# A recurrent block (autocorrelation gather and LoRA feed-forward) on one core: earlier gather sums, searches ahead of outputs, LoRA's copies and w2's sums in other places

## The chip, the cores and the metric

The kernel runs on one NeuronCore of a Trainium2 chip. The metric is the device time in microseconds (us). Five engines work side by side, each through its own instructions in their written order: TensorE (PE, matrix products), VectorE (DVE), ScalarE (ACT), GpSimd (POOL, which also issues the indirect DMAs) and SyncE (SP, which issues the other DMAs). They wait for one another by semaphores.

## The reference

`x` is (2, 2048, 1024) in f32, that is 4096 rows of 1024.

```
xn = (x - mean) / sqrt(var + 1e-5)                    # per row
corr = irfft(|rfft(xn)|^2)                            # autocorrelation of each row
weights, delay = top_k(corr, 6)
s = sum_k softmax(weights)_k * roll(xn, -delay_k)     # "aggregate"
w(q) = tile(q, (1, 4));  lin(v) = v @ w.T + 0.5 * v @ A.T @ B.T   # rank 2
g = silu( lin2( silu(lin1(xn)) * lin3(xn) ) )         # hidden width 2752
out = x + s * g
```

The weights are tiled four times along their input, so the kernel folds the four parts of the input (or, for w2, of the output columns) before it multiplies.

## The kernel before

**Macros and steps.** The rows are taken in 8 macros of 512 rows (4 blocks r of 128). Each macro goes through 15 steps. Steps 0 to 9 (`up`) make the gated products of the hidden width: 5 chunks c in two pairs, with the matmuls of L556 into PSUM banks gu, a silu on ACT (L561), a product with the other half on DVE (z, L563) and sums over z on POOL (zf, L566 and L568). Step 10 (`up_rest`) makes the last, half-wide chunk: gu by L585 and L592, z by ACT (L602) and DVE (L603), sums on POOL (L607, L608) and DVE (L609). Steps 11 and 13 (`down_head`, q = 0 and 1: two row blocks each) and 12 and 14 (`down_tail`) make the down product y from seven sub-products p1 to p7 (L641) of sums of weights (B, and T1 to T4) and sums of zf (S1, S2, S4, made by `mix` on POOL, L633 to L636), then the `plain` products of the half-wide chunk (L651), silu (L722), the product with s (DVE, L723), the sum with x (POOL, L724) and the store (L725). Four y banks are used for each q; the fourth, y11, takes the bank that gu of the second unit of step 10 had, and p7 is the first product written to it.

**What runs beside.** While a macro's products run, the next macro is prepared: loads of x, statistics (L185 to L193), norm (L200 to L207, then yc and bcs, L145 and L134), a save of xn into a scratch in DRAM (twice in a row, so that a roll is one contiguous read), `turn` (transposes on PE, L230), at steps 9 and 10 `power` (the transform: waves fe and fo on PE, L384; ec, e2 and o2 on ACT; bT and its like on DVE, L394, and POOL, L395 and L398), and at steps 11 to 14 `lags` (corr by L426 to L443) and `search` (the six largest, their places and exponentials; L451, L453 on DVE, e by L462 on POOL). A search gives six gathers of `Gathers`: at most four rolls are in flight, by indirect DMA from POOL (L486), in five buffers. The first roll of a row block is scaled on ACT (L500), the other five are added on DVE (L503).

**What sets the order.** The program is written out by hand: program order is the order on each engine. `plan` gives each step lists of calls: `pre` ahead of its products, `mid` between them, `half` behind `mid`, and `end`; and `sums[p]`, how many gather sums are made at half and at the end of step p. `Gathers.begin` issues rolls ahead of each step and behind the sums at half. In `down_tail`, `between` stands between the outputs of the first and the second half of the columns. Two sums of each macro's r = 3 come behind its outputs, in step 1 of the next macro.

**Other names of the change.** `mix_weights`: four subtractions over w2 on POOL (L163 to L166), once, in macro 0. `lora_mid` (L611): four small sums into the half-wide chunk's zf and a copy on ACT (L619). `flush`: matmuls u of LoRA (L539) that were put off. `again` and `lora_spread`: one matmul u (L258), four copies on ACT and three DMAs on SP (rows, second) for the next macro. Buffer rings: tags "x" and "s" have three 128x1024 buffers each.

Sums at (half, end) before: steps 0 to 14 of the later macros (0,0) (1,1) (1,0) (1,0) (1,0) (1,0) (1,0) (2,1) (2,1) (2,1) (0,0) (1,0) (1,0) (2,1) (3,0).

Of the kernel before, what the change touches and what calls it, by code (L numbers as in the profile page):

```python
# [68 lines left out]
def block_kernel(ctx: ExitStack, tc: tile.TileContext, x, w13t, w0t, w5t, w2t, a13, b13, b5, a2t, tf, ti, pick, out):  # L69
# [78 lines left out]
    def fold_lora(nat):  # L148
# [11 lines left out]
    B = lambda k, n: w2_sb[:, :4, :].rearrange("p (a k) l -> p a k l", k=2)[:, :, k, n * 512 : (n + 1) * 512]  # L160
    T1, T2, T3, T4 = B(0, 1), t_sb[:, 0], t_sb[:, 1], t_sb[:, 2]
    mix_weights = [
        lambda: nc.gpsimd.tensor_tensor(T3, B(1, 1), B(0, 1), ALU.subtract),  # L163
        lambda: nc.gpsimd.tensor_tensor(T1, B(0, 1), B(0, 0), ALU.subtract),
        lambda: nc.gpsimd.tensor_tensor(T2, B(1, 1), T1, ALU.subtract),
        lambda: nc.gpsimd.tensor_tensor(T4, B(1, 0), T2, ALU.subtract),  # L166
    ]


# [305 lines left out]
    class Gathers:  # L475
# [16 lines left out]
        def sum(self, count):  # L492
            for _ in range(count):
                if not self.flying:
                    self.begin()
                st, r, k, g = self.flying.pop(0)
                w = st.w[:, r, k : k + 1]
                if k == 0:
                    s = self.s[st.m, r] = p3.tile([P, L], F32, tag="s", name=f"s_{st.m}_{r}")
                    nc.scalar.activation(s, g, AF.Copy, scale=w)  # L500
                else:
                    s = self.s[st.m, r]
                    nc.vector.scalar_tensor_tensor(s, g, w, s, ALU.mult, ALU.add)  # L503


    class Ffn:
# [69 lines left out]
        def up_rest(self, mid, half):  # L576

            st = self.st
            self.seed(4 * FULL + 2)
            self.seed(4 * FULL + 3)  # L580
            accs = [self.accs.pop(4 * FULL + j) for j in range(4)]
            for pair in range(2):
                js = (2 * pair, 2 * pair + 1)
                for j in js:
                    nc.tensor.matmul(  # L585
                        accs[j], lhsT=w5_sb[:, 1, j, :], rhs=st.yT[:, 1, :], start=False, stop=False, skip_group_check=True
                    )

                for j in js:
                    for wi, y in enumerate((st.yT[:, 0, :], st.yU)):  # L590
                        at = slice(64 * wi, 64 * wi + 64)
                        nc.tensor.matmul(  # L592
                            accs[j][at, :], lhsT=w5_sb[:, 0, j, at], rhs=y, start=False, stop=True, skip_group_check=True
                        )
                if pair == 0:
                    self.flush()
                    mid()
                    half()
            zs = self.zs[FULL] = []
            for j, acc in enumerate(accs):  # L600
                z = p5.tile([P, NR], F32, tag="z", name=f"z_{self.m}_{FULL}_{j}")
                nc.scalar.activation(z[:64, :], acc[:64, :], AF.Silu)  # L602
                nc.vector.tensor_tensor(z[:64, :], z[:64, :], acc[64:, :], ALU.mult)  # L603
                zs.append(z)
            self.late.append(lambda: self.a2(FULL, zs, 64))
            last = self.sum_of(FULL)
            nc.gpsimd.tensor_tensor(last[:64, :], zs[0][:64, :], zs[1][:64, :], ALU.add)  # L607
            nc.gpsimd.tensor_tensor(last[:64, :], last[:64, :], zs[2][:64, :], ALU.add)  # L608
            nc.vector.tensor_tensor(last[:64, :], last[:64, :], zs[3][:64, :], ALU.add)  # L609

        def lora_mid(self):  # L611

            self.flush()
            last = self.zf[FULL]
            for j in range(4):
                nc.vector.scalar_tensor_tensor(
                    last[0:2, :], self.u2[32 * j : 32 * j + 2, :], 0.5, last[0:2, :], ALU.mult, ALU.add
                )
            nc.scalar.copy(last[64:, :], last[:64, :])  # L619
# [41 lines left out]
        def down_head(self, q, mid, half):  # L661

            self.q, self.xs = q, {}
            for i, n in ((0, 0), (1, 0), (0, 1)):
                self.load_x(i, n)
            self.rc = [slice((2 * q + i) * P, (2 * q + i + 1) * P) for i in range(2)]
            A = lambda i, k: [self.zf[2 * a + k][:, self.rc[i]] for a in range(2)]
            S = [[t[:, 2 * a + q, :] for a in range(2)] for t in self.S]
            both = lambda t: [t[:, a, :] for a in range(2)]
            self.forms = [  # L670
                list(zip(lhs, both(rhs)))
                for lhs, rhs in (
                    (A(0, 0), B(0, 0)), (A(0, 1), B(1, 0)), (S[2], B(1, 1)), (A(1, 1), T4), (S[0], T1), (S[1], T2), (A(1, 0), T3),
                )
            ]
            p1_, p2_, p3_, p4_, p5_, p6_, p7_ = self.forms

            self.ys = [full(f"y_{self.m}_{2 * q + i}_{n}") for n in range(2) for i in range(2)]
            y00, y10, y01, y11 = self.ys
            self.add_to(y01, p1_, True)  # L680
            nc.scalar.copy(y00, y01)
            self.add_to(y11, p7_, True)
            self.p7 = p5.tile([P, NR], F32, tag="z", name=f"p7_{self.m}_{q}")
            nc.scalar.copy(self.p7, y11)
            self.add_to(y01, p6_)
            nc.vector.tensor_tensor(y10, y01, self.p7, ALU.add)
            if q == 0:
                self.lora_mid()
            mid()
            half()  # L690
            self.add_to(y00, p2_)
            self.add_to(y00, self.plain(0, 0))
# [35 lines left out]
    def plan(m, st, nxt, after, gathers, ffn_next):  # L728

        pre, mid, half, end = ([[] for _ in range(STEPS)] for _ in range(4))  # L730
        first = m == 0
        sums = [(1, 0)] * 7 + [(1, 2)] * 3 + [(1, 1), (0, 0), (2, 1), (2, 1), (0, 0)]
        sums[10] = (0, 0)
        sums[0], sums[1] = (0, 0), (1, 1)
        sums[7:10] = [(2, 1)] * 3
        sums[11:] = [(1, 0), (1, 0), (2, 1), (3, 0)]
        between = lambda: None
        if first:
            sums = [(0, 0)] * 7 + [(1, 1), (2, 1), (1, 2), (2, 2), (2, 1), (1, 0), (2, 1), (3, 0)]
            for p, f in enumerate(mix_weights):  # L740
                half[6 + p].append(f)
            mid[0].append(st.odd_first)
            pre[1].append(lambda: st.power(2))
            mid[1].append(lambda: st.power(3))
            for r in range(RT):
                look(st, r, mid[2 + r], end[2 + r], gathers)
            mid[2 + RT].append(st.weights)
            for c in range(2, FULL + 1):
                pre[(0, 0, 1, 3)[c - 2]].append(lambda c=c: load_first(c))
                end[2 * c - 3].append(lambda c=c: lessen_part(c))  # L750
        else:
            end[0].append(st.weights)
        if nxt is not None:
# [17 lines left out]
            mid[9].append(lambda: nxt.power(1))  # L771
            pre[10].append(lambda: nxt.power(2))
            mid[10].append(lambda: nxt.power(3))
            pre[11].extend([nxt.again, nxt.lora_spread])
            for r in range(RT):
                look(nxt, r, mid[MID + 1 + r], end[MID + 1 + r], gathers)
            mid[STEPS - 1].insert(0, lambda: ffn_next.seed(0, (0,)))
            between = lambda: (ffn_next.seed(0, (1,)), ffn_next.seed(1, (0,)))
            end[STEPS - 1].insert(0, lambda: ffn_next.seed(1, (1,)))
        for a in range(2):  # L780
            end[8 + a].append(lambda a=a: ffns[m].mix(a))
        if after is not None:
            pre[MID + 2].append(lambda: after.load(0))
            pre[MID + 4].append(lambda: after.load(1))
# [25 lines left out]
    with tc.manual_schedule():  # L810
# [73 lines left out]
        for m in range(macros):  # L884
# [3 lines left out]
            for p in range(STEPS):  # L888
                for f in pre[p]:
                    f()  # L890
                gathers.begin()
                middle = lambda p=p: [f() for f in mid[p]]

                def others(p=p):
                    gathers.sum(sums[p][0])
                    if sums[p][0]:
                        gathers.begin()
                    for f in half[p]:
                        f()

                if p < MID:
                    ffn.up(p // 2, p % 2, middle, others)
                elif p == MID:
                    ffn.up_rest(middle, others)
                else:
                    q, part = divmod(p - MID - 1, 2)
                    if part == 0:
                        ffn.down_head(q, middle, others)
                    else:
                        s = lambda i, q=q: gathers.s[m, 2 * q + i]  # L910
                        ffn.down_tail(middle, others, s, between if q else lambda: None)
                gathers.sum(sums[p][1])
                for f in end[p]:
                    f()
# [111 lines left out]
```

## Time and profile before

| | |
|---|---|
| runs | 1174.82, 1176.18, 1178.7 us (median 1176.18) |
| profiled execution | 1179.55 us, span of its instructions 1177.7 us |
| mean granted PE clock | 0.987 |
| VectorE L503 (gather sums) | 158, 237.1 us busy, 1.28 us median |
| POOL L486 (rolls) | 192, 240.1 us busy |
| PE L556 (up products) | 1280 matmuls, 626.7 us busy |
| macro 1, 216.9 to 358.5 us | 141.6 us, PE busy 138.72 |
| macro 7, 1046.0 to 1177.7 us | 131.7 us, PE busy 121.39 |

A row of a timeline has the start, the length (of a run of equal instructions), the engine, the line, the operation with the names of its output and inputs, shapes, and a count; in square brackets stands how long the engine sat idle before it and what ended that. A list of waits has, for an engine's line and the one that released it, the total, the number and the longest. A row of a window table has, behind its stretch in us, its length, then busy time and count of PE, weight loads, DVE, ACT and POOL, then the granted PE clock, the DMA share and GB/s. A matmul of 512 columns starts 0.429 us behind the last one in a dense stretch; its listed length overlaps the next.

### The profile page before, as it was taken

What the parts mean: (1) busy time and instruction counts of PE and PEld (TensorE: products, weight loads), DVE (VectorE), ACT (ScalarE), POOL (GpSimd) and SP (SyncE); (2) the same over time, 40 slices, a digit from 0 to 9 for tenths busy, and PEclk for the clock granted to TensorE, in tenths of its full rate; (3) what the DMA queues carried; (4) which work ended last, traced back from release to release, by engine and by line L of the source; (5) the groups of instructions that cost most, each with busy time, mean ns of one, the idle gap of its engine ahead of it and who ended that gap; (6) DMA issues with size and microseconds to landing.
All of it is one profiled execution on the core that took longest, in us unless ns stands there. A gap on an engine that the chain in (4) does not pass through costs nothing.

```text
span 1177.7 us, 11263 instructions
## 1 busy us (share of the span) xinstructions
PE 1120.5 (95%) x3476; PEld 472.5 (40%) x3476; DVE 758.2 (64%) x1122; ACT 619.5 (53%) x1077; POOL 779.3 (66%) x659
## 2 busy tenths in 40 slices
PE   5999879999999999899999999999999999999996
PEld 4344234443343434344343433434334443344432
DVE  5589467765586647766487655866557865574454
ACT  4656523666346663465635665355643666345531
POOL 4667967548666585666956568665767648665663
PEclk9999989999999999999999999999999999999998
DMA  9841357543475334654356544554446543363335
GB/s 364 372 163 54 92 203 239 198 143 111 156 225 203 130 124 160 230 187 143 107 174 217 178 159 144 172 191 173 144 134 219 198 146 117 133 206 126 112 120 187
DMA packets 64915, 201.77 MB, mean 171 GB/s; under 512 B 7612, under 2 KB 7868, under 8 KB 64088
## 3 DMA queue, kind: packets, MB, share of 16 engines
q0 software_dynamic: 27648, 100.68, 26.7%
q1 hardware_dynamic: 37208, 100.39, 23.6%
q8 instruction: 27, 0.44, 0.1%
q14 instruction: 32, 0.26, 0.1%
HBM read 150.65 MB, written 50.39 MB: 171 GB/s over the span
## 4 chain that ended last, share of the span: by engine, by line
PE 50%; POOL 19%; DMA 11%; issue 9%; ACT 6%; DVE 4%; SPq 0%; POOLq 0%; DVEq 0%; ACTq 0%
PE gu L556 37%; POOL roll L486 5%; DMA x<-in_x 5%; DMA out<-x 4%; PE y L641 3%; POOL x L724 3%; PE u L539 3%; PE t L230 2%; DMA roll<-scr,lag 2%; POOL e L462 2%; ACT gu L527 2%; POOL bT L395 1%; POOL zf L568 1%; PE fe L381 1%; PE fo L381 1%
## 5 line engine op out<-in xcount | busy, mean ns | idle before, releaser
L556 PE MATMUL gu<-yT,w_sb 128*128 128x512 f32 x960 | 462.2, 603 | 0.0
L486 POOL DMA_INDIRECT roll<-scr,lag x192 | 240.1, 1250 | 51.4 <-issue 30.5
L556 PEld LDWEIGHTS gu<-yT,w_sb 128*128 128x128 f32 x960 | 177.2, 191 | 234.5 <-issue 213.2
L503 DVE SCALAR_TENSOR_TENSOR s<-roll,w,s 128x1024 f32<-128x1024 f32 x158 | 237.1, 1501 | 17.5 <-DMA roll<-scr,lag 14.9
L563 DVE TENSOR_TENSOR z<-z,gu 128x512 f32<-128x512 f32 x160 | 109.3, 684 | 173.1 <-PE gu L556 116.5
L534 ACT ACTIVATE gu<-second,b_sb 128x512 f32<-128x512 f32 x320 | 209.0, 685 | 18.9 <-DVE z L563 17.6
L568 POOL TENSOR_TENSOR zf<-zf,z 128x512 f32<-128x512 f32 x80 | 127.8, 1598 | 79.5 <-DVE z L563 78.2
L561 ACT ACTIVATE z<-gu 128x512 f32<-128x512 f32 x160 | 95.0, 594 | 146.6 <-PE gu L556 146.4
L556 PE MATMUL gu<-yU,w_sb 128*128 128x512 f32 x320 | 164.5, 596 | 1.5 <-ACT gu L534 1.5
L724 POOL TENSOR_TENSOR x<-g,x 128x512 f32<-128x512 f32 x62 | 84.9, 1379 | 72.2 <-DMA x<-in_x 46.4
L641 PE MATMUL y<-w_sb,zf 128*128 128x512 f32 x256 | 121.4, 596 | 0.0
L566 POOL TENSOR_TENSOR zf<-z,z 128x512 f32<-128x512 f32 x40 | 57.9, 1447 | 85.8 <-DVE z L563 85.7
L556 PEld LDWEIGHTS gu<-yU,w_sb 128*128 128x128 f32 x320 | 61.1, 192 | 80.1 <-issue 73.0
L462 POOL TENSOR_TENSOR e<-euler,e 128x6 f32<-128x6 f32 x32 | 46.7, 1461 | 69.0 <-DVE e L461 69.0
L723 DVE TENSOR_TENSOR g<-s,g 128x512 f32<-128x512 f32 x64 | 55.2, 885 | 39.0 <-ACT g L722 37.6
L722 ACT ACTIVATE g<-y 128x512 f32<-128x512 f32 x64 | 36.3, 594 | 80.7 <-POOL x L724 41.2
L641 PEld LDWEIGHTS y<-w_sb,zf 128*128 128x128 f32 x256 | 46.9, 191 | 57.9 <-issue 57.0
L641 PE MATMUL y<-t_sb,zf 128*128 128x512 f32 x128 | 64.0, 624 | 5.7 <-DVE z L603 5.7
L444 ACT COPY corr<-corr 128x511 f32<-128x511 f32 x32 | 19.8, 617 | 83.9 <-DVE corr L443 83.9
L641 PE MATMUL y<-w_sb,S 128*128 128x512 f32 x128 | 61.9, 606 | 2.0 <-DVE y L698 2.0
L539 PE MATMUL u<-z,a_sb 128*2 128x512 f32 (+1 forms) x384 | 51.0, 591 | 1.9 <-DVE z L563 1.9
L206 DVE TENSOR_TENSOR a<-x 128x512 f32<-128x512 f32 x28 | 33.1, 1183 | 26.7 <-ACT x L200 26.7
(180 smaller groups left out, 1506.0 us busy)
## 6 DMA issues: line engine op xcount, KB each, us to landing
scr<-x SPq DMA_DIRECT2D x64, 512.0 KB
x<-in_x SPq DMA_DIRECT2D x32, 512.0 KB
x<-in_x SPq DMA_DIRECT2D x64, 256.0 KB
out<-x SPq DMA_DIRECT2D x64, 256.0 KB
w_sb<-in_w13t SPq DMA_DIRECT2D x5, 1024.0 KB
second<-rows SPq DMA_DIRECT2D x14, 256.0 KB
w_sb<-in_w2t SPq DMA_DIRECT2D x1, 3072.0 KB
roll<-scr,lag POOLq DMA_INDIRECT x192, 5.2
```

The source lines that it names most:

```text
L462: nc.gpsimd.tensor_tensor(e, bass.AP(euler.tensor, euler.offset, [list(euler.ap[0]), [0, TOP]]), e, ALU.pow)
L486: nc.gpsimd.indirect_dma_start(out=g, out_offset=None, in_=st.scratch[r].rearrange("p (n o) -> (p n) o", o=1), in_offset=bass.IndirectOffs ...
L503: nc.vector.scalar_tensor_tensor(s, g, w, s, ALU.mult, ALU.add)
L534: nc.scalar.activation(acc, self.st.second[:, wi, :], AF.Copy, scale=b13_sb[:, c, q : q + 1])
L539: nc.tensor.matmul(self.u2[32 * j : 32 * j + 2, :], lhsT=a2_sb[:rows, 4 * c + j, :], rhs=z[:rows, :], start=(c == 0), stop=(c == FULL),)
L556: nc.tensor.matmul(acc, lhsT=w13_sb[:, c, 2 * j + wi, k, :], rhs=y, start=False, stop=(k == 1), skip_group_check=True,)
L561: nc.scalar.activation(z, accs[0], AF.Silu)
L563: nc.vector.tensor_tensor(z, z, accs[1], ALU.mult)
L566: nc.gpsimd.tensor_tensor(self.sum_of(c), zs[0], zs[1], ALU.add)
L568: nc.gpsimd.tensor_tensor(self.zf[c], self.zf[c], z, ALU.add)
L641: nc.tensor.matmul(acc, lhsT=lhs, rhs=rhs, start=(first and a == 0), stop=True, skip_group_check=True)
L724: (nc.vector if last else nc.gpsimd).tensor_tensor(xt, g, xt, ALU.add)
```

## The change

Five things are moved.

- The gather sums get new lists. In the later macros no sum is left in steps 11 to 14; step 10 gets two at half and two at its end. One sum of r = 3 stays in step 1 of the next macro.
- The sum s of r = 3 takes a buffer of x's ring.
- The searches move: r = 0 from the end of step 11 to the middle of step 12, r = 1 from the end of step 12 to `between` of step 12, r = 3 from the end of step 14 to half of step 14; r = 2 stays.
- `lora_mid` goes from ahead of `mid` in the first `down_head` to the end of step 11, and takes the last sum of step 10 with it; `again` and `lora_spread` go from ahead of step 11 to its end.
- The four subtractions of `mix_weights` go from POOL, half of steps 6 to 9, to DVE, the ends of steps 8 and 9.

```diff
     mix_weights = [
-        lambda: nc.gpsimd.tensor_tensor(T3, B(1, 1), B(0, 1), ALU.subtract),
...
+        lambda: nc.vector.tensor_tensor(T3, B(1, 1), B(0, 1), ALU.subtract),
...
                 if k == 0:
-                    s = self.s[st.m, r] = p3.tile([P, L], F32, tag="s", name=f"s_{st.m}_{r}")
+                    s = self.s[st.m, r] = p3.tile([P, L], F32, tag="x" if r == RT - 1 else "s", name=f"s_{st.m}_{r}")
...
-            nc.vector.tensor_tensor(last[:64, :], last[:64, :], zs[3][:64, :], ALU.add)
 
         def lora_mid(self):
 
-            self.flush()
-            last = self.zf[FULL]
+            last, z = self.zf[FULL], self.zs[FULL][3]
+            nc.vector.tensor_tensor(last[:64, :], last[:64, :], z[:64, :], ALU.add)
...
-            if q == 0:
-                self.lora_mid()
+            self.flush()
             mid()
             half()
...
-        sums = [(1, 0)] * 7 + [(1, 2)] * 3 + [(1, 1), (0, 0), (2, 1), (2, 1), (0, 0)]
-        sums[10] = (0, 0)
-        sums[0], sums[1] = (0, 0), (1, 1)
-        sums[7:10] = [(2, 1)] * 3
-        sums[11:] = [(1, 0), (1, 0), (2, 1), (3, 0)]
-        between = lambda: None
+        sums = [(0, 0), (1, 1), (1, 0), (1, 1), (1, 0), (1, 1), (1, 1), (2, 1), (2, 1), (2, 2), (2, 2)] + [(0, 0)] * 4
+        between = {MID + 2: [], MID + 4: []}
         if first:
-            sums = [(0, 0)] * 7 + [(1, 1), (2, 1), (1, 2), (2, 2), (2, 1), (1, 0), (2, 1), (3, 0)]
-            for p, f in enumerate(mix_weights):
-                half[6 + p].append(f)
+            sums = [(0, 0)] * 6 + [(0, 1), (1, 1), (2, 1), (2, 2), (2, 3), (2, 1), (2, 0), (2, 1), (0, 0)]
+            for i, f in enumerate(mix_weights):
+                end[8 + i // 2].append(f)
...
-            pre[11].extend([nxt.again, nxt.lora_spread])
+            end[MID + 1].extend([nxt.again, nxt.lora_spread])
             for r in range(RT):
-                look(nxt, r, mid[MID + 1 + r], end[MID + 1 + r], gathers)
+                look(nxt, r, mid[MID + 1 + r], (mid[MID + 2], between[MID + 2], end[MID + 3], half[MID + 4])[r], gathers)
             mid[STEPS - 1].insert(0, lambda: ffn_next.seed(0, (0,)))
-            between = lambda: (ffn_next.seed(0, (1,)), ffn_next.seed(1, (0,)))
+            between[MID + 4].append(lambda: (ffn_next.seed(0, (1,)), ffn_next.seed(1, (0,))))
             end[STEPS - 1].insert(0, lambda: ffn_next.seed(1, (1,)))
         for a in range(2):
             end[8 + a].append(lambda a=a: ffns[m].mix(a))
+        end[MID + 1].append(ffns[m].lora_mid)
...
-                        ffn.down_tail(middle, others, s, between if q else lambda: None)
+                        ffn.down_tail(middle, others, s, lambda p=p: [f() for f in between[p]])
```

More of the change, by code (lines that the diff above doesn't have):

```diff
@@ L162, in block_kernel @@
     mix_weights = [
-        lambda: nc.gpsimd.tensor_tensor(T3, B(1, 1), B(0, 1), ALU.subtract),
-        lambda: nc.gpsimd.tensor_tensor(T1, B(0, 1), B(0, 0), ALU.subtract),
-        lambda: nc.gpsimd.tensor_tensor(T2, B(1, 1), T1, ALU.subtract),
-        lambda: nc.gpsimd.tensor_tensor(T4, B(1, 0), T2, ALU.subtract),
+        lambda: nc.vector.tensor_tensor(T3, B(1, 1), B(0, 1), ALU.subtract),
+        lambda: nc.vector.tensor_tensor(T1, B(0, 1), B(0, 0), ALU.subtract),
+        lambda: nc.vector.tensor_tensor(T2, B(1, 1), T1, ALU.subtract),
+        lambda: nc.vector.tensor_tensor(T4, B(1, 0), T2, ALU.subtract),
     ]
```

## The prediction

> **What bounds the kernel now.** I read the page's busy shares first, then who waited on TensorE (PE), then tables of windows, then the timelines around the longest waits.
>
> ```profile
> PE 1120.5 (95%) x3476; PEld 472.5 (40%) x3476; DVE 758.2 (64%) x1122; ACT 619.5 (53%) x1077; POOL 779.3 (66%) x659
> ```
>
> PE is the bound: it idles 57 us of 1177.7. A change that adds or removes no matmul can move only those 57 us, and the matmuls that ran at half clock. The list of waits on PE says where:
>
> ```profile
> engine line waited for: us in total, times, longest us
> PE t L230 <- DVE yc L145: 15.2, 6, 3.0
> ...
> PE y L641 <- DVE z L603: 5.7, 1, 5.7
> PE y L641 <- ACT y L681: 3.6, 6, 0.6
> PE fo L384 <- DVE bT L394: 2.2, 2, 1.7
> ```
>
> The first row is the largest that recurs: once per boundary between two macros (217.0, 358.5, 499.2, 640.8, 782.6, 924.6 us). It costs more than its 15.2 us:
>
> ```profile
> 516.00:522.00 6.00, 6.00 (x27) 2.64 (x25) 3.46 (x7) 4.32 (x9) 5.55 (x6) 1.00 0.49 167
> 217.00:221.50 4.50, 4.50 (x13) 2.50 (x14) 4.50 (x7) 2.74 (x6) 2.74 (x2) 0.62 0.70 251
> 499.20:504.70 5.50, 5.48 (x15) 2.59 (x16) 5.50 (x9) 3.86 (x8) 3.71 (x2) 0.69 0.58 208
> ```
>
> Last but two in a row is the granted clock: 1.00 in a dense stretch, 0.62 and 0.69 just behind a stall. From the last matmul ahead of the stall to the next u (L539) the six boundaries take 9.61, 7.53, 10.0, 8.81, 9.70 and 7.81 us in the timeline; the same instructions take 4.83 us in an undisturbed step (516.58 to 521.41). The six differences sum to 24.5 us, 4.1 each.
>
> Why yc is late, from the timelines of DVE, POOL and PE at the boundary of 640.8 us:
>
> ```profile
> 623.01 1.28 DVE L503 SCALAR_TENSOR_TENSOR s<-roll,w,s 128x1024 f32<-128x1024 f32 x1 [1.25 <-DMA roll<-scr,lag]
> 624.21 1.28 DVE L723 TENSOR_TENSOR g<-s,g 128x512 f32<-128x512 f32 x2
> ```
> ```profile
> 624.11 0.99 POOL L486 DMA_INDIRECT roll<-scr,lag  x1 [0.30 <-issue]
> 625.13 2.71 POOL L724 TENSOR_TENSOR x<-g,x 128x512 f32<-128x512 f32 x2
> ...
> 634.06 1.27 POOL L724 TENSOR_TENSOR x<-g,x 128x512 f32<-128x512 f32 x1 [4.32 <-DMA x<-in_x]
> 635.29 1.35 POOL L462 TENSOR_TENSOR e<-euler,e 128x6 f32<-128x6 f32 x1
> ```
> ```profile
> 640.77 1.06 PE L230 MATMUL t<-ident,yc 128*128 128x128 f32 x4 [2.11 <-DVE yc L145]
> ```
>
> ACT had the first g at 620.1, but DVE multiplies it at 624.21 behind three sums; POOL is behind four rolls; the x of the last output block can be loaded only when the first block's store has left its buffer (store issued 626.65, landed 630.77, load landed 633.9), and POOL waits 4.32 us for it with e L462 and the norm's rstd L191 queued behind. Then rstd 636.63, x L200 637.57, yc 640.15, PE 640.77.
>
> **Part by part: the sums and searches at the boundary.** The new list leaves steps 11 to 14 without a sum, and only three rolls (the first of the next macro) there; the searches of r=2 and r=3, and with them POOL's e, go ahead of the outputs. Removed ahead of the last g: three sums and 1.64 us of DVE waits for rolls, 3 x 1.28 + 1.64 = 5.5 us, of which the moved search gives back 2.75 (L451 1.21 + L453 1.22 + small ones); POOL loses four rolls (4 x 1.24 with gaps) and gains one e (1.35). g starts near 621.3, the chain behind it comes at least 2.8 us earlier, and e no longer follows it, another 1.3: 4 us for a stall of 2.0 to 3.0. So it goes, and yc has a little over 1 us in hand. Late next would be ACT's z (L561), which PE doesn't await there. Gain: **-24.5 us**.
>
> **The sums at step 10.** They do not vanish; each macro from 1 on now has two sums in step 10 between DVE's last bT (L394) and the four z (L603), and two behind these; before it had none. Step 10 now, macro 4, DVE and PE:
>
> ```profile
> 582.68 0.69 DVE L394 TENSOR_TENSOR bT<-ec,fo 128x512 f32<-128x512 f32 x1 [7.51 <-ACT o L393]
> 583.40 2.52 DVE L603 TENSOR_TENSOR z<-z,gu 64x512 f32<-64x512 f32 x4
> ```
> ```profile
> 583.01 1.88 PE L641 MATMUL y<-w_sb,zf 128*128 128x512 f32 x4
> 584.84 1.96 PE L641 MATMUL y<-t_sb,zf 128*128 128x512 f32 x4
> 587.40 1.98 PE L641 MATMUL y<-t_sb,S 128*128 128x512 f32 x4 [0.61 <-ACT y L681]
> ```
>
> The product at 584.84 (p7) writes y11, in the bank that the second z of L603 must have read; that z ends at 584.70, just in time. bT can't come sooner: it waits for ACT's o L393, that for POOL's L395 (580.75 to 582.0), and the built program keeps POOL's order up to there with as many rolls. With two sums of 1.28 between, the second z ends at 584.70 + 2.6 = 587.3, p7 starts at 587.4. I know this from macro 0, which has two sums there already:
>
> ```profile
> 146.15 2.60 DVE L503 SCALAR_TENSOR_TENSOR s<-roll,w,s 128x1024 f32<-128x1024 f32 x2
> 148.78 2.52 DVE L603 TENSOR_TENSOR z<-z,gu 64x512 f32<-64x512 f32 x4
> ```
> ```profile
> 150.23 3.75 PE L641 MATMUL y<-t_sb,zf 128*128 128x512 f32 x4 [5.69 <-DVE z L603]
> ```
>
> The diff also takes u (L258, 0.96 us of PE) away from ahead of p1, so PE is ready for p7 at 583.9 and idles 3.5 us. Against before: p7 2.6 later; p6 no longer waits 0.6 for ACT (its four LoRA copies moved); u's 0.96 comes behind: net +2.8 us to p5 (593.86 becomes 596.7), 6 macros, **+16.8**.
>
> Then the clock. Macro 0's 5.69 us idle were followed by eight matmuls at 0.855 instead of 0.429 us: 3.4 lost. The boundaries' 3.0 idle lost about 2.0. For 3.5 I take 2.0, the nearer (ends 0 and 3.4): **+12.0**. Here a rule speaks against the rows. The Trainium skill (TensorE: Matmul & The Clock Gate, "Part 1: The HAM clock gate") says that the clock halves after at least one idle window of about 3.4 us, a free-running one. By it the boundaries' 2.1 to 3.0 us shouldn't halve the clock, so their removal gives only the start-to-start loss of 16.2, while p7's 3.5 us could: 3.4 us at half clock lose 1.7, 10.2 in six. The sum of these parts would be -16.2 + 16.8 + 10.2 = +10.8; by the rows it is -24.5 + 16.8 + 12.0 = +4.3. The trace has 0.62 behind an idle 2.70, so I go by the rows.
>
> One more sum in step 9 puts bT of the third wave later beside fo L384, with a margin of some 0.4 us: 0 to 1.7 (the row above) each, I take 0.2, **+1.2**. POOL's z sums (L607, L608) shift with z by 2.6; the row sum they feed is needed at 599 by rest L651, and lora_mid now makes it by about 597 behind y00: nothing, with 2 us of cover. The a2 of z_5 (u L539, 589.32) follows p6 and finds z at 588.5.
>
> **The moves of LoRA and spread.** again and spread: one matmul, four copies, three DMAs on SP, from before to behind step 11's products; the x loads go ahead of rows and second on SP. Seeds of the next macro need second only 35 us later. Nothing beyond what is counted.
>
> **s of r=3 in x's ring.** The third x of the next macro but one is loaded at pre of step 1 and now waits for s_3's last sum, in the same step; behind it on SP nothing that is due before step 3. Its norm is some 16 us later, the delay 2 to 3: 0 (bounds 0 and +3 in all).
>
> **w2's sums to VectorE.** POOL loses 4 subtractions in macro 0 (2.35 + 2.39 + 2.37 + 2.36 = 9.5), DVE gains four of 1.28 to 2.34 (its own 128x1024 rows, alone and beside POOL) at the ends of steps 8 and 9. T's are read from 150 on: hidden. Macro 0's bT path on POOL comes 2.4 earlier, p7 (5.69 idle) about 1.5; an ACT seed stall of 1.5 behind POOL's x at 205 goes; three sums ahead of lora_mid and the fo stall cost some. Total **-4** (bounds -8 and +2).
>
> **Macro 7** has no next macro, so no waves (fe, fo) between its products. Its k=0 sum of r=3 is ACT's, at the end of step 9, ahead of the seeds of gu_5_2 and gu_5_3. Its roll is issued at POOL 1122.2 and lands 4.1 to 5.2 later, near 1127; gu_5_2 starts now at 1126.45, and would start 3 to 4 us later, plus 1 of clock. The tail loses its three sums, worth 2.1 us. Net **+2.2** (0 to +6).
>
> Sum: -24.5 + 16.8 + 12.0 + 1.2 - 4 + 2.2 = **+3.7 us**. The profiled execution took 1179.55 (span 1177.7 and 1.85 around), 3.4 above the median of the runs; I carry the difference to the median: 1176.18 + 3.7 = **1179.9**.
>
> **Rivals.** *Faster (0.23)*: the wait at p7 doesn't halve the clock, and macro 7's roll is in time. -24.5 + 16.8 + 1.2 - 4 + 0 = -10.5, so 1165.7. For it: 2.20 and 2.50 us of idle at two boundaries cost only 2.7 and 3.0 in all. Against: 3.5 exceeds each of the six. *Slower (0.13)*: the two sums at step 10 run beside POOL's L395, L398 and rolls and take 2.8 each (133.62 us has one of 2.79 beside L398) instead of 1.28. p7 then waits 6.5 us, the clock loss is macro 0's 3.4: +3.0 + 1.4 more in each of six, 1179.9 + 26 = 1206. It decides from about 4 us for the pair; against it, macro 0's pair took 2.60 beside rolls. *The boundary stall stays (0.07)*: the moved searches hold g as the sums did; then +24.5: 1204. *It doesn't do what it says (0.07)*: one sum of each macro still falls into step 1 of the next, as two do now; if the whole only shuffles hidden work, 1176.
>
> **Chances.** Main case 0.50, 1172 to 1187; the others as above. Against the 0.3% (3.5 us) that a measurement can tell from no change: the main case splits into 0.25 within, 0.24 slower, 0.01 faster; with the others faster 0.24, same 0.32, slower 0.44. The range leaves out the two cases near 1205 and goes 3.7 below the faster rival for macro 0's lower bound: 1162 to 1192; the likeliest case's own is 1172 to 1187.
>
> **What would show it.** Right: no PE wait on yc; a wait of y on z L603 of 3 to 4 us in macros 1 to 6, with a granted clock near 0.7 behind it; macro windows 0.5 to 1 us longer; a PE wait near 1127 on a seed. Wrong: z L603 in time, or the new wait in another place, such as y00 behind lora_mid.

## The result, and the profile after

The changed kernel takes 1193.58 us (median of 4 runs, 1191.93 to 1195.02) against 1175.83 (4 runs, 1174.82 to 1178.7): a ratio of 1.0147, interval 1.0122 to 1.0171. That is 17.8 us slower, 1.6 us outside the range; the forecast was 3.7 us slower. The profiled execution took 1191.93 us, with a span of 1190.1 and a mean granted clock of 0.977 (before: 0.987).

The busy shares hardly move, and PE is still the bound, with 62 us of idle time. The list of waits on PE of the changed kernel has other names:

```profile
PE 1128.0 (95%) x3476; PEld 477.4 (40%) x3476; DVE 773.6 (65%) x1127; ACT 617.8 (52%) x1077; POOL 799.1 (67%) x655
```
```profile
PE y L640 <- DVE z L603: 23.2, 6, 3.9
...
PE fo L384 <- DVE bT L394: 5.6, 2, 3.8
PE gu L585 <- ACT gu L527: 4.9, 1, 4.9
PE y L650 <- DVE zf L615: 4.0, 1, 4.0
```

The six waits on yc (15.2 us) are gone. Six waits on z L603 (23.2) stand in their place, one in each of macros 1 to 6. One on a seed stands in macro 7 (4.9; a seed is the product on ACT, L527 or L534, that fills a gu bank ahead of its matmuls), and macro 0 has bT (5.6 in two; the one of 1.7 was there before) and lora_mid's zf (4.0).

The boundary between macros 3 and 4, from the timelines of POOL, DVE and PE, answers to the one shown of before at 640.8 us. (Counted from 0, the step 10 that the prediction shows at 583 us as macro 4's is macro 3's.) Line 722 is before's 724:

```profile
622.91 1.70 POOL L462 TENSOR_TENSOR e<-euler,e 128x6 f32<-128x6 f32 x1 [3.87 <-DVE e L461]
...
631.41 1.27 POOL L722 TENSOR_TENSOR x<-g,x 128x512 f32<-128x512 f32 x1 [1.74 <-DMA x<-in_x]
```
```profile
636.91 0.47 DVE L145 SCALAR_TENSOR_TENSOR yc<-a,rest 128x256 f32<-128x256 f32 x1
```
```profile
640.30 0.60 PE L230 MATMUL t<-ident,yc 128*128 128x128 f32 x4
```

e is done ahead of the outputs, the last x waits 1.74 us for its load instead of 4.32, and yc is written at 637.4. PE comes to it 2.9 us later, without a gap in front.

Step 10 of macro 3, DVE and then PE:

```profile
578.98 0.69 DVE L394 TENSOR_TENSOR bT<-ec,fo 128x512 f32<-128x512 f32 x1 [6.25 <-ACT o L393]
579.59 2.60 DVE L503 SCALAR_TENSOR_TENSOR s<-roll,w,s 128x1024 f32<-128x1024 f32 x2
582.22 2.52 DVE L603 TENSOR_TENSOR z<-z,gu 64x512 f32<-64x512 f32 x4
```
```profile
583.66 3.75 PE L640 MATMUL y<-t_sb,zf 128*128 128x512 f32 x4 [3.88 <-DVE z L603]
```

The two sums stand between bT and z, as in the program; p7 waits 3.88 us, and its four matmuls then take 3.75 us in all where four took 1.96 before. The window table gives the clock behind the wait in this stretch, 0.52:

```profile
583.60:590.00 6.40, 6.33 (x8) 2.52 (x8) 5.40 (x4) 0.59 (x1) 6.23 (x3) 0.52 0.50 152
```

### The profile page after: what moved, and what is told of

It is laid out like the page before. It is cut to its first block, busy times and chain, and to the rows that moved or that the text cites. A ratio compares the mean times of both kernels' runs of the same rounds, so it can differ in the third digit from the quotient of the medians.

```text
span 1190.1 us, 11264 instructions
## 1 busy us (share of the span) xinstructions
PE 1128.0 (95%) x3476; PEld 477.4 (40%) x3476; DVE 773.6 (65%) x1127; ACT 617.8 (52%) x1077; POOL 799.1 (67%) x655
## 3 DMA queue, kind: packets, MB, share of 16 engines
q1 hardware_dynamic: 37208, 100.39, 23.2%
## 4 chain that ended last, share of the span: by engine, by line
PE 62%; POOL 19%; issue 8%; DVE 6%; DMA 3%; ACT 2%; SPq 0%; POOLq 0%; DVEq 0%; ACTq 0%
PE gu L556 34%; PE y L640 18%; POOL roll L486 5%; PE y L650 3%; PE u L539 3%; POOL zf L568 2%; POOL pwy L398 2%; DVE s L503 2%; POOL zf L566 2%; PE t L230 1%; DMA x<-in_x 1%; PE o L426 1%; PE e L426 1%; POOL S L633 1%; POOL S L632 1%
## 5 line engine op out<-in xcount | busy, mean ns | idle before, releaser
L556 PE MATMUL gu<-yT,w_sb 128*128 128x512 f32 x960 | 457.5, 598 | 0.0
L503 DVE SCALAR_TENSOR_TENSOR s<-roll,w,s 128x1024 f32<-128x1024 f32 x159 | 249.0, 1566 | 41.9 <-ACT s L500 23.4
L534 ACT ACTIVATE gu<-second,b_sb 128x512 f32<-128x512 f32 x320 | 208.2, 685 | 6.3 <-DVE z L563 5.6
L566 POOL TENSOR_TENSOR zf<-z,z 128x512 f32<-128x512 f32 x40 | 65.4, 1634 | 67.8 <-DVE z L563 61.8
L640 PE MATMUL y<-t_sb,zf 128*128 128x512 f32 x128 | 69.9, 674 | 23.2 <-DVE z L603 23.2
L721 DVE TENSOR_TENSOR g<-s,g 128x512 f32<-128x512 f32 x64 | 43.0, 711 | 44.8 <-ACT g L720 44.6
L640 PEld LDWEIGHTS y<-t_sb,zf 128*128 128x128 f32 x128 | 25.2, 211 | 51.9 <-POOL bT L395 28.5
```

The costliest lines, as they stand in the source:

```text
L534: nc.scalar.activation(acc, self.st.second[:, wi, :], AF.Copy, scale=b13_sb[:, c, q : q + 1])
L556: nc.tensor.matmul(acc, lhsT=w13_sb[:, c, 2 * j + wi, k, :], rhs=y, start=False, stop=(k == 1), skip_group_check=True,)
L566: nc.gpsimd.tensor_tensor(self.sum_of(c), zs[0], zs[1], ALU.add)
L640: nc.tensor.matmul(acc, lhsT=lhs, rhs=rhs, start=(first and a == 0), stop=True, skip_group_check=True)
```

## The experiments

Each is timed beside the kernel before; "before" in a ratio is those runs. Their medians differ, from 1171.4 to 1175.3 us, so differences of times between two batches are good to some 4 us.

**Sums behind z.** Theory A is the mechanism of the prediction at its measured size.

```diff
-  (2, 1), (2, 1), (2, 2), (2, 2)] + [(0, 0)] * 4
+  (2, 1), (2, 1), (2, 2), (0, 4)] + [(0, 0)] * 4
```

> The changed kernel with step 10's four sums all behind z of the half-wide chunk (none ahead of it). Theory A (the two sums between bT and z hold y11's bank, and that wait with its half-clock matmuls costs 4.7 to 6.1 us in each of macros 1 to 6): the wait of y on z L603 is gone there, no wait of PE on yc comes back, and the time falls by about 34 us, to 1157 to 1163. Rival B (VectorE is simply late after step 10, wherever the sums stand): the wait moves to y's additions or to rest, and the time stays above 1180.

Measured: 1179.3 us (1178.68 to 1181.15), ratio 1.0042 (1.0028 to 1.0057). 14 us below the changed kernel, less than half of what theory A asked. The half-clock matmuls behind p7 are gone in macros 1 to 6, but three smaller waits stand in each:

```profile
PE y L640 <- DVE y L685: 9.6, 6, 1.6
...
PE y L640 <- DVE z L603: 8.1, 6, 1.4
PE e L426 <- ACT yU L269: 6.4, 7, 1.0
```

The first is seen in the timelines of DVE and PE, macro 3:

```profile
579.59 8.99 DVE L503 SCALAR_TENSOR_TENSOR s<-roll,w,s 128x1024 f32<-128x1024 f32 x4
588.62 0.70 DVE L685 TENSOR_TENSOR y<-y,p 128x512 f32<-128x512 f32 x1
```
```profile
589.37 1.98 PE L640 MATMUL y<-w_sb,S 128*128 128x512 f32 x4 [1.60 <-DVE y L685]
```

Four sums behind z take 8.99 us, 2.25 each instead of 1.28, and y's addition comes late behind them. So both theories hold a part: the place ahead of z is what brings the half clock, and step 10 has no room for four sums in any of the three orders tried (this one, the change's and the next).

**One sum ahead.** `(1, 3)` in place of `(2, 2)` in step 10.

> The changed kernel with one sum ahead of z in step 10 and three behind it. Theory A: the wait of y on z is one sum (1.3 us) shorter, 2.5 to 2.7 us, and its half-clock matmuls stay or fall in some macros: 1178 to 1187. Rival B: as the changed kernel. If the clock has a threshold above 2.7 us of idle time: 1172 or below.

Measured: 1175.19 us, ratio 1.0006 (0.9992 to 1.002): 18 us below the changed kernel (16 to 17 by the ratios) for one sum of 1.28 us in each of six macros, moved behind z. That is below theory A's bracket and above that of a sharp threshold. p7 waits 2.5 us in all six. In a dense stretch p7 is followed by the first corr matmul (L426) 4.57 us later. This takes 1.70, 1.69, 1.50, 0, 1.69 and 0 us longer here, and 1.61, 1.69, 3.02, 3.04, 3.06 and 3.06 in the changed kernel, whose wait is 3.9. The window behind p7 at 582.49 in this kernel, with a clock of 0.76:

```profile
582.40:588.80 6.40, 6.31 (x18) 2.43 (x19) 6.33 (x5) 0.58 (x1) 6.17 (x3) 0.76 0.55 168
```

**Old lists.** All of the change but its lists (and x's ring):

```diff
-  tag="x" if r == RT - 1 else "s"
+  tag="s"
-  sums = [(0, 0), (1, 1), (1, 0), (1, 1), ...                 # and macro 0's list
+  sums = [(0, 0), (1, 1), (1, 0), (1, 0), ... (3, 0)]         # before's
```

> The changed kernel with the lists of sums of the kernel before, and s of r=3 in its own ring again: only the searches, LoRA's moves and w2's sums on VectorE are left of the change. Theory A: the wait on yc at the boundary stays (three sums and four rolls are still in step 14, and the search of r=3 is now ahead of g): 15 to 25 us of it in the list of waits, no wait of y on z beyond macro 0, time 1172 to 1184. Rival C (the searches' move alone removes the boundary wait): 1150 to 1158.

Measured: 1162.97 us, ratio 0.9892 (0.9867 to 0.9918). Theory A fell here: no wait on yc, although three sums and four rolls stand in step 14. Rival C has the mechanism; its bracket ended 5 us too low, and a new wait takes part of the gain. The wait on PE, and the place at the boundary behind macro 3 (DVE, ACT, PE):

```profile
PE gu L556 <- ACT gu L534: 10.1, 7, 2.1
```
```profile
612.39 1.22 DVE L451 MAX8 top<-corr 128x8 f32<-128x1024 f32 x1
```
```profile
618.43 0.60 ACT L720 ACTIVATE g<-y 128x512 f32<-128x512 f32 x1 [7.35 <-POOL x L722]
```
```profile
620.88 1.13 PE L556 MATMUL gu<-yU,w_sb 128*128 128x512 f32 x2 [2.13 <-ACT gu L534]
```

Sums and search together hold DVE until 615.25; the first outputs are late, ACT waits for a g buffer, and the seed of the next macro's gu stands behind g on ACT.

**Lists only.** The kernel before with the new lists and x's ring.

> The kernel before with the new lists of sums and s of r=3 in x's ring, and nothing else of the change. Theory A: the boundary wait goes with the sums, the wait of y on z comes, 2.6 to 3.0 us in each of six macros since u stands ahead of p1: 1178 to 1190. Rival C (the searches' move removes the boundary wait): both waits stand, above 1198.

Measured: 1203.39 us, ratio 1.0242 (1.0214 to 1.027), above theory A's bracket. The yc wait is absent here too, so rival C's reason for a high time is not it. The waits are these:

```profile
PE y L641 <- DVE z L603: 23.6, 7, 5.7
PE o L426 <- ACT oc L430: 11.4, 7, 1.8
```

Besides z, corr's matmuls wait for ACT, since lora_mid's copy (L619) stands ahead of oc. This wait is absent in the changed kernel, where lora_mid has left step 11's head. The changed kernel takes 9.8 us less than this one (1203.4 to 1193.6), but the searches and w2 are moved there as well: what LoRA's moves alone are worth under the new lists was not measured.

In macros 1 to 6 the wait on z is 3.0 us here, and the way from p7 to the first corr matmul is the dense 4.57 us in four of them, 6.12 and 7.56 in the other two. A wait half a microsecond longer than that of one sum ahead was followed by the half clock less often.

**Searches only**, and **LoRA's moves only**, on the kernel before.

> The kernel before with only the four searches moved as in the change. Theory D, formed on the earlier runs (the boundary wait is owed to e and the search of r=3 standing behind POOL's last x, and their move alone removes it; VectorE's search ahead of g then makes ACT's g, and the seeds behind it, late by 1.2 to 2.3 us): no wait on yc, a wait of gu on the seed of L534 in each macro, 1158 to 1165. Rival E (the gain with the old lists came from LoRA's copies leaving step 11): above 1170 here.

> The kernel before with only LoRA's moves: lora_mid, again and lora_spread at the end of step 11. Theory D: the boundary wait of about 15 us stays, the wait of y on ACT goes (-3.6), u (0.96) no longer stands ahead of p1 and p7 waits about 0.9 for z, and rest of macro 0 waits for lora_mid: 1172 to 1179. Rival E: 1160 to 1168.

Measured: searches 1167.19 us, ratio 0.9929 (0.9905 to 0.9953), no wait on yc, 12.7 us in seven waits on L534's seed; LoRA 1177.77 us, ratio 1.0021 (1.0004 to 1.0038), the yc wait still 15.3 us. Theory D holds in its mechanism; the searches' time is 2 us above its bracket. Rival E falls. The list of searches only has:

```profile
PE gu L556 <- ACT gu L534: 12.7, 7, 3.4
```

**A list for the last macro.** The changed kernel with

```diff
+        if nxt is None:
+            sums[9:11] = [(2, 1), (0, 5)]
```

> The changed kernel with a list of its own for the last macro: one sum at the end of step 9 and five at the end of step 10, none ahead of z, so that ACT's first sum of r=3 stands behind the seeds. If the seed's wait (4.9 us and half-clock matmuls) is what the last macro lost: 4 to 7 us below the changed kernel, 1187 to 1190. If the last macro only pays the same elsewhere (z, rest or the output's end): within 2 us of the changed kernel.

Measured: 1193.65 us, the changed kernel's time. In the changed kernel ACT stood at the sum of a roll that had not landed, with the seeds behind it (timelines of POOL, ACT, PE):

```profile
1131.75 1.77 POOL L486 DMA_INDIRECT roll<-scr,lag  x1
```
```profile
1136.94 1.15 ACT L500 ACTIVATE s<-roll,w 128x1024 f32<-128x1024 f32 x1 [6.42 <-DMA roll<-scr,lag]
```
```profile
1139.57 3.53 PE L585 MATMUL gu<-yT,w_sb 128*128 128x512 f32 x4 [4.91 <-ACT gu L527]
```

With the new list that wait is gone, and this one is in its place:

```profile
PE y L640 <- DVE y L685: 5.7, 1, 5.7
```

DVE waits 4.06 and 2.46 us for rolls in step 10, with y's addition behind. In both placements, on ACT and on VectorE, the last macro pays for asking for sums earlier than its rolls land.

**w2's subtractions back on POOL**, in the changed kernel.

> The changed kernel with the four subtractions of w2 back on POOL at half of steps 6 to 9. If they are what holds bT and with it fo in macro 0 (3.8 us and some half-clock matmuls): that wait falls under 2 us and the time is 2 to 5 us below the changed kernel, 1188.5 to 1191.5. If POOL is the longer way (its rolls and z sums behind 2.4 us each): the wait moves to y on z in macro 0, and the time is the changed kernel's or up to 4 us above it.

Measured: 1193.82 us, the changed kernel's time. The waits on bT fall from 5.6 to 2.9, and a wait of 6.5 on z in macro 0 comes: the second branch of the expectation. In time this part of the change is worth nothing that these runs can tell.

**One search only.** The kernel before with r = 3 alone moved.

> The kernel before with one search moved: r=3 from the end of step 14 to half of step 14, behind the three sums there. Theory D: this one move carries what all four moved searches gave (they took 8 us off), with the wait on yc gone and the seed's wait in its place: 1164 to 1170. If the earlier searches of r=0 and 1 count as well: 1170 to 1175 with part of the yc wait left.

Measured: 1181.34 us, ratio 1.0071 (1.0047 to 1.0095). Neither branch gave the time. The yc wait is gone, so r = 3 alone carries that; but the seed's wait is 20.8 us in seven, more than the 12.7 with all four searches moved:

```profile
PE gu L556 <- ACT gu L534: 20.8, 7, 5.0
```

At the end of macro 3, with r = 1 where it was, its e on POOL (611.43 us) still stands behind an x that waits 2.02 us for its load, and pushes the rolls: the last three sums of step 14 wait 1.83 us for them (0.57 and 1.26), against 0.85 with all four moved. g and the seed behind it are later by about that, and PE's wait there is 2.77 us instead of 1.84. The half clock adds to it: the granted clock is 0.86 from 628 to 640 us, and 1.00 in the same place (625 to 637) with all four moved. The other boundaries were not followed.

**Step 10's sums in steps 11 to 13.** The changed kernel with

```diff
-  (2, 2), (2, 2)] + [(0, 0)] * 4
+  (2, 2), (0, 0), (1, 0), (1, 0), (2, 0), (0, 0)]
```

> The changed kernel with step 10's four sums in steps 11 (one), 12 (one) and 13 (two) instead, for macros 1 to 7; the rest as changed. If the place of these four sums is what the new lists cost: no wait of y on z beyond 1.5 us in each macro, no wait of y on its additions, no half clock there, and 30 to 38 us below the changed kernel, 1155 to 1163. If sums in steps 11 to 13 bring back a wait at the boundary or in the down product: 1168 or more.

Measured: 1161.02 us, ratio 0.9906 (0.9885 to 0.9927), 32.6 us below the changed kernel (28 by the ratios) for moving four sums. The clock behind p7, where the wait is now 1.32 us, is full:

```profile
572.20:578.60 6.40, 6.38 (x26) 2.91 (x27) 2.30 (x5) 1.30 (x3) 6.09 (x5) 1.00 0.61 221
```

**Spread further**, and **macro 0's subtractions earlier**.

> As the last one, with step 9's fourth sum also in step 13, w2's subtractions on POOL, and macro 0's step 10 with four sums behind z and none ahead. The seed's wait of the last macro (4.9 us) goes, macro 0's waits on bT and z shrink by 2 to 6 us, no step 14 sum: 1148 to 1157. If macro 7's or macro 0's waits only move, as the last macro's did: 1157 to 1163.

> As the spread version before it (1157.8), with two things of macro 0 changed: w2's subtractions on VectorE at the ends of steps 6 and 7 (not 8 and 9, where they stood ahead of bT), and one sum instead of three ahead of lora_mid in step 11. If the place of the subtractions decides: the waits on bT (2.9), on z in macro 0 (4.0) and on lora_mid's zf (3.5) fall by half or more together, 1150 to 1155. If they are limited by the rolls and waves, whatever engine subtracts: 1156 to 1159.

Measured: 1157.78 us, ratio 0.9876 (0.9854 to 0.9897), and 1157.78 us, ratio 0.9861 (0.9837 to 0.9885). The spread version beats both kernels. In the last one, macro 0's waits on bT (2.9 to 1.7) and on z (4.0 to about 1) fall and the one on lora_mid's zf (3.5) goes. But the one on ACT's y in step 11 grows from 0.9 to 2.9 us, and one in step 13 from 1.7 to 7.6, where VectorE waits 5.97 us for a roll ahead of y's addition:

```profile
PE y L640 <- DVE y L696: 7.6, 1, 7.6
```

So in this order macro 0 pays in step 13 for its rolls what it gained before; whether another order escapes that was not tried.

## Why the prediction was wrong

The waits came where the prediction placed them, and the two mechanisms, sums at the boundary and sums ahead of z, were right. What failed is the sum: four of its terms were mis-sized, one was not there, and a gain read from one profile was carried to the median. By terms, between the two profiled executions:

- **The boundary wait goes: right, its reason half right.** The prediction ascribed the late yc to sums, rolls and the search's e together. Either alone is enough: lists only and searches only both have no wait on yc. With the searches alone the wait turns into the seed's (12.7 us); with the sums gone as well it does not.
- **Its worth, -24.5: right for the profile, too much for a median execution.** From p5 of a macro to step 10 of the next, the five boundaries behind macros 1 to 5 are 19.9 us shorter in the profile after; the prediction's rows for these five sum to 19.7. But the profile before (1179.55 us) stands 3.7 us above its median, and the one after (1191.93) 1.7 below its own. These 5.4 us are the difference between the 12.4 us of the profiled pair and the 17.8 of the medians. Over 25 executions of the kernel before in one later batch, a mean clock lower by 0.001 goes with 0.9 us more; the profile has 0.987 and the median of that batch 0.990, which would make some 2.8 of the 3.7 us half clock, an estimate. That they sat in those very boundaries is inferred, not shown.
- **p7 and what follows, +16.8: the mechanism right, a little short.** The predicted idle time was 3.5 and the measured 3.88, because bT came 0.5 us later relative to p1. From p1 to p5, without the clock's part, the six macros grew by 18.3 us, 1.5 more.
- **"For 3.5 I take 2.0": mis-sized.** Behind p7 the clock cost 1.6 to 3.1 us, 15.5 in six instead of 12.0.
- **Macro 7, +2.2: mis-sized.** From its step-10 gu to the end it took 60.2 us instead of 55.9, +4.3. The roll was issued at 1131.75, 1.4 us later than taken, and landed 5.2 us later; PE waited 4.9 instead of 3 to 4, and its next gu ran at half clock.
- **Macro 0, -4: mis-sized.** bT waits 3.8 and lora_mid's zf 4.0 us, each with half-clock matmuls. Up to macro 1's step 10 the profile gains 5.8 us, of which 4.8 are the boundary at 217. So macro 0 itself gained about 1.
- **fo in macros 1 to 6, +1.2: wrong.** No such wait occurred.

Predicted 3.7; with +1.5, +3.5, +2.1, +3 and -1.2 it is 12.6 against the 12.4 of the profiled pair; the rest of the 17.8 is the choice of executions.

The rule against the rows: by the Trainium skill (TensorE: Matmul & The Clock Gate, "Part 1: The HAM clock gate") one idle window of about 3.4 us, free-running, would have given 1.7 us in each macro behind p7, an estimate from the page's figure. The runs show up to 3.1 behind 3.9 us of idle time, and 1.5 to 1.7 in four of six cases behind 2.5. At the five boundaries the start-to-start times alone would have given 13.3 us, and 19.9 came. The rows were nearer in both terms, and still too low in the first. With the rule the whole forecast would have been +10.2, nearer to the 12.4 than the rows' +3.7; that would have been luck, since its two terms err in opposite directions.

The faster rival was wrong in its premise, a wait of 3.5 us that leaves the clock alone. The rival of stretched sums has its mechanism in the runs (2.25 us each, with POOL's L398 beside them), but behind z, where it was not placed; ahead of z the pair took 2.60, as macro 0's had.

What the change lost in all is the place of four sums: 32.6 us come back when they leave step 10, and of the 17.8 us nothing is left.

## What to carry to other kernels

A short instruction put between a late input and the instruction that frees a PSUM bank costs its length on TensorE, and more where the half clock follows the gap: moving the second sum of 1.28 us behind z saved 18.4 us in six macros, 3.1 each. Before moving work to an earlier step, look for the step in which the engine's queue is already just in time, and leave that one alone. And a gain that contains half-clock matmuls is to be read from several executions, not from one profile.

## What the runs showed of the hardware

- The half clock behind p7's wait, by the time to the first corr matmul, varied with the length and from case to case: nothing lost behind 1.3 to 1.7 us (six of six, step 10's sums in steps 11 to 13); nothing in two and 1.5 to 1.7 us in four behind 2.5 (one sum ahead); nothing in four, 1.6 and 3.0 us in one each behind 3.0 (lists only); 1.4 to 3.1 us in all eighteen behind 3.8 to 3.9 (the changed kernel, the last macro's list, w2 on POOL). Its length alone does not decide.
- The spread of a kernel's times went with its waits: 1156.9 to 1158.1 and 1159.8 to 1161.4 (four executions each) for two kernels with full clock behind p7 in all of macros 1 to 6, and 1171.5 to 1182.9 (twenty; 7.4 us among the first four) with six waits on yc (LoRA's moves only). With the longer wait on z, four executions lay within 1.1 us (w2 on POOL), 3.1 (the changed kernel) and 3.9 (the last macro's list).
- 128x1024 sums on VectorE took 1.28 us alone and 2.25 in a row of four beside POOL's additions.
